# Five edits to a fused gated cross-attention and stream-mixing kernel: squares behind their loads, the high half of x from x itself, maxima one patch earlier, the last map in halves, and idle weights as output buffers

## The chip, the cores and the metric

The kernel runs on one core of one Trainium2 chip, as one program. The metric is device time in microseconds (us) of one execution. Before the change three runs took 1733.73, 1724.82 and 1726.72 us, so the median is 1726.72 us. One further execution was profiled; it took 1734.36 us, and the profile's span, from the first to the last instruction, is 1732.6 us.

The engines are named as in the profile: PE is the matrix engine (PEld its weight loads), DVE the vector engine, ACT the scalar engine, POOL the GpSimd engine and SP the queue that issues nearly all DMAs. Each of them works through its own instructions strictly in the order in which the program lists them.

## The reference

The input `x` is 8 batches of 512 rows by 2048 columns. Two blocks follow each other, each added to `x` with a gate:

```python
x = x + tanh(g_xattn) * xattn(layernorm(x), ctx, mask, Wq, Wk, Wv, Wo, biases)
x = x + tanh(g_ffn)   * ffn(layernorm(x), W_res, W_pre, W_post, bases, gate, W_branch)

def xattn(qk, v, masks):                 # per batch: 16 patches of 128 columns
    q, k = Wq @ qk + bq, Wk @ qk + bk    # 256 x 128 each, 8 heads of 32
    val  = Wv @ v + bv
    attn = softmax(q_h^T k_h / sqrt(32)) # 128 x 128 per head
    o    = gelu(val_h attn^T)            # exact gelu
    return (Wo @ o + bo) * masks

def ffn(x):                              # per row: 2048 columns = 4 streams of 512
    xn    = x * rsqrt(mean(x*x) + eps)
    H_res = sinkhorn(xn @ W_res.T + base, 50 iterations, tau 0.1)  # 4 x 4 per row
    H_pre, H_post = softmax(...), softmax(...)                     # 4 per row
    H_res = (1-g) * I + g * H_res
    y     = (sum_n H_pre[n] * x_n) @ W_branch
    return H_res @ x_streams + H_post * y
```

## The kernel before

**Steps.** The work is laid out in 128 steps `t`, one for each patch of 128 columns; four steps make a block `n` of 512 columns (`p` is the step within the block), four blocks a batch of 512 x 2048. The string `ORDER = "MeoaMgPlsMMvSMpOM"` is the order of the parts within a step, and `act(c, t)` runs the part of one letter. The parts that the change touches or that stand next to them:

- `s`: `smax(t + AHEAD)`, with `AHEAD = 3`. Eight products of a patch's queries and keys go into PSUM (L341), DVE takes the row maxima (L344, one reduction over 1024 columns), the maxima are split in two halves, turned by PE (L349), copied by ACT (`mh`, L351) and written by a DMA into rows 97 and 98 of the patch's query tile (L354). There they act as the subtracted maximum.
- `e`: `expo(t)`. The scores again, transposed and with the maxima in (L616), and their exponential on ACT (L618). `a`: `attv(t - 1)`, sums and products with the values. `g`, `o`, `O`: `outp`, gelu, output product, residual (L648 to L695).
- `p`: `proj(n + 2)`, the query and key projections. At `p == 0` the four 128 x 512 tiles of the block are normalised: POOL writes `xn = x * rstd + nb` (L271), ACT makes the 16-bit high half `h` from `xn` (L276), POOL the low half `l = xn - h` (L278). Afterwards twelve products for each of four row groups `m` (L289 to L291), and the result is written to DRAM (`qd`, L295).
- `stack(m)`: six DMAs (L308) and a mask row (L313) read `qd` back into one of `NS = 3` pairs of tiles `QS`, `KS`; one pair holds two patches. `stack(2n + 3)` is in the step `p == 2` (letter `P`), `stack(2n + 4)` at the end of the step `p == 3` (letter `p`).
- `S`: one step of `stats(b)`, the mean and variance of a later batch. Five pieces load 16 tiles of the transposed input (L577) and multiply them (L565); then the squares of x - mean are summed. For this 16 tiles are loaded (L597) and squared by ACT (L598), all sixteen in two pieces, each load followed by its square. All 32 tiles of a batch go through four buffers (`xTt`). With `EARLY = 4`, `stats(b)` starts at step t = 16 b - 20 for the batches from 2 on; batch 1 starts at t = 0.
- After a batch's last block, `ffn` makes the maps of all its 512 rows: a chain of 49 sweeps, each a product, a row sum and a reciprocal, twice (L865 to L875). For the batches 0 to 6 the two products of a sweep are on POOL and the rest on DVE; for batch 7 all is on DVE. `SPLITS` says in how many parts of the rows each operation of the chain is done.
- `mix`: the maps are applied, one quarter (128 rows) at a time. `mixv` does it on ACT, DVE and POOL (L964 to L975). `mixp` does it on PE; it is used for the twelve quarters that `PE_MIX` lists, of batches 4 to 7, and runs after step 128. Its outputs go from PSUM through a buffer `wp` (ACT, L1028) to DRAM (L1029). The buffers of `wp` are taken in turn from two pools: one buffer `eh` and two buffers `e32`.

**What sets the order.** The source gives the dependencies and an order of preference. When the program is built, a scheduler walks a simulated timeline and fixes the list of instructions of every engine, SP's list of DMAs included. So an edit in one part can shift the place of instructions of other parts. In the program before, the maxima of patch k + 3 always begin ahead of the scores of patch k + 1.

Of the kernel before, what the change touches and what calls it, by code (L numbers as in the profile page):

```python
# [9 lines left out]
F32 = mybir.dt.float32  # L10
# [3 lines left out]
AF = mybir.ActivationFunctionType  # L14
# [5 lines left out]
P = 128  # L20
# [5 lines left out]
BLK = 512  # L26
NBLK = S // BLK
# [4 lines left out]
NS = 3  # L32
HI = 1000
XPRE_POOL = lambda b: b < 7
AHEAD = 3
LXP = 1
SK_POOL = lambda b: b < 7
CT_ACT = False
XS_ACT = False
POOLMIX = lambda i, j: j == 1 and i > 0  # L40
BUF_GP = 1
BUF_OP = 1
BUF_XHP = 4
BUF_XNP = 2
BUF_XTP = 4
BUF_CTP = 2
BUF_QDP = 3
# [3 lines left out]
LASTN = 1  # L51
LASTM = 3
YS = True
EARLY = 4
LAGS = (30,) * 8
NV = 2
MIXN = 2
# [4 lines left out]
BUF_W = 2  # L62
# [3 lines left out]
BUF_EP = 2  # L66
BUF_XPRE = 1
PSTEPS = (0,1,1,2)
SP0 = 1
XH_POOL = lambda c: False  # L70
CAP = 1.0
NORM0 = True
D_MH = 0
# [3 lines left out]
D_ST = 0  # L77
BUF_XP = 20
PE_MIX = ((), (), (), (), (3,), (0, 1, 2, 3), (0, 1, 2, 3), (1, 2, 3))
SPLITS = (1, 1, 1, 1, 1, 1, 1, 1)  # L80
CHAINS = ((0,), (1,), (2,), (3,), (4,), (5,), (6,), (7,))
BUF_SK = 2
PE_IN = ((), (), (), (), (), (), (), ())
# [16 lines left out]
def gated_xattn_mhc_kernel(  # L100
# [21 lines left out]
    V, A, G, T, SY = nc.vector, nc.scalar, nc.gpsimd, nc.tensor, nc.sync  # L122
# [6 lines left out]
    def ctile(shape, dt, name):  # L129
        return const.tile(shape, dt, tag=name, name=name)  # L130
# [16 lines left out]
    WqkH = ctile([P, 4, 512], F16, "WqkH")  # L147
    WqkL = ctile([P, 4, 512], F16, "WqkL")
    Wv = ctile([P, 4, DK], F32, "Wv")
# [35 lines left out]
    xsp = ctx.enter_context(tc.tile_pool(name="xsp", bufs=2))  # L185
    xnp = ctx.enter_context(tc.tile_pool(name="xnp", bufs=BUF_XNP))
    xhp = ctx.enter_context(tc.tile_pool(name="xhp", bufs=BUF_XHP))
# [3 lines left out]
    ep = ctx.enter_context(tc.tile_pool(name="ep", bufs=BUF_EP))  # L191
# [6 lines left out]
    VF = [ctile([P, 2, DK], F32, f"VF{i}") for i in range(NV)]  # L198
# [5 lines left out]
    def defer(k, tag, fn):  # L204
        if k == 0:
            fn()
        else:
            late.append([k, fn, tag])
# [6 lines left out]
    def flush(which):  # L215
        for e in [e for e in late if which(e)]:
            late.remove(e)
            e[1]()
# [3 lines left out]
    rstd1 = {}  # L222
    nb1 = {}
# [28 lines left out]
    def finish_stats(b, nm, var):  # L252
        r = rsqrt(ln0, var, eps_ln, 4, "ln1")
        nb = ln0.tile([P, 4], F32, tag="nb1", name="nb1")
        V.tensor_tensor(nb, nm, r, ALU.mult)  # L255
        nmean[b], rstd1[b], nb1[b] = nm, r, nb
# [4 lines left out]
    def proj(n):  # L261

        b, k = divmod(n, NBLK)
        xt = xtile[n]
        hs, ls = [], []
        for c in range(4):
            xn = xnp.tile([P, BLK], F32, tag="xn", name="xn")
            if n == 0 and c > 1:
                A.activation(xn, xt[c], AF.Identity, scale=rstd1[b][:, c : c + 1], bias=nb1[b][:, c : c + 1])
            else:  # L270
                G.tensor_scalar(xn, xt[c], rstd1[b][:, c : c + 1], nb1[b][:, c : c + 1], ALU.mult, ALU.add)  # L271
            h = xhp.tile([P, BLK], F16, tag="xh", name="xh")
            if XH_POOL(c):
                G.tensor_copy(h, xn)
            else:
                A.copy(h, xn)  # L276
            l = xhp.tile([P, BLK], F16, tag="xl", name="xl")
            (V if n == 0 and c > 1 else G).tensor_tensor(l, xn, h, ALU.subtract)  # L278
            hs.append(h)
            ls.append(l)  # L280
        if NORM0:
            yield
        qd = qdp.tile([2, 4, 2, P, BLK], F16, tag="qd", name="qd")
        qds[n] = qd
        for m in range(4):
            ps = ps_p.tile([P, BLK], F32, tag="p", name="qk")
            ms = slice(m * P, (m + 1) * P)
            for c in range(4):
                T.matmul(ps, WqkH[:, c, ms], hs[c], start=(c == 0), stop=False)  # L289
                T.matmul(ps, WqkH[:, c, ms], ls[c], start=False, stop=False)  # L290
                mm = T.matmul(ps, WqkL[:, c, ms], hs[c], start=False, stop=(c == 3))  # L291
            ev = evp.tile([P, 2, BLK], F16, tag="ev", name="ev")
            ae = A.activation(ev[:, 0, :], ps, AF.Identity, bias=bqs[:, m : m + 1])  # L293
            ve = V.scalar_tensor_tensor(ev[:, 1, :], ps, bqs[:, m : m + 1], ev[:, 0, :], ALU.add, ALU.subtract)  # L294
            defer(D_QD, "qd", lambda m=m, ev=ev: SY.dma_start(qd[m // 2, 0:2, m % 2].rearrange("t p s -> p t s"), ev))  # L295
            if n == LASTN and m == LASTM:
                last.update(pe=mm, act=ae, dve=ve)
            yield
# [252 lines left out]
    fp = ctx.enter_context(tc.tile_pool(name="fp", bufs=2))  # L551
# [5 lines left out]
    def stats(b):  # L557

        lgs = xsp.tile([P, 512], F32, tag="lgs", name="lgs", bufs=1)
        for q4 in range(5):  # L560
            if q4 > 0:
                flush(lambda e: e[2] == "st")
                lg = ps_t.tile([P, 512], F32, tag="t", name="lgx")
                for g in range(4):
                    T.matmul(lg[32 * g : 32 * g + 32, :], Wm[:, 4 * q4 - 4 + g, :], xts[g], start=True, stop=True)  # L565
                if q4 == 1:
                    V.tensor_copy(lgs, lg)
                else:
                    V.tensor_tensor(lgs, lg, lgs, ALU.add)
            if q4 < 4:  # L570
                xts = []

                def ld(q4=q4, xts=xts):
                    for g in range(4):
                        xt_ = xtp.tile([P, 512], F32, tag="xTt", name="xTt")
                        k = 4 * q4 + g
                        SY.dma_start(xt_, xT[b, k * P : (k + 1) * P, :])  # L577
                        xts.append(xt_)

                defer(D_ST, "st", ld)  # L580
                yield 1
        rp = ps_t.tile([P, 4, 32], F32, tag="t", name="rawp")
        for c in range(4):
            T.matmul(rp[:, c, :], lgs[:, c * P : (c + 1) * P], sel, start=True, stop=True)
        rw = lnp.tile([P, 4, 32], F32, tag="rawx", name="rawx")
        V.tensor_copy(rw, rp)
        rawx[b] = rw
        if b == 0:
            return
        nm = ln0.tile([P, 4], F32, tag="nmean", name="nmean")  # L590
        V.tensor_scalar(nm, rw[:, :, NM], -1.0 / S, None, ALU.mult)
        yield 1
        sq = lnp.tile([P, 4, NBLK], F32, tag="sq1", name="sq1")
        for c in range(4):
            for k in range(NBLK):
                xs = xtp.tile([P, BLK], F32, tag="xTt", name="xs")
                (A if XS_ACT else SY).dma_start(xs, x[b, c * P : (c + 1) * P, k * BLK : (k + 1) * BLK])  # L597
                A.activation(xs, xs, AF.Square, bias=nm[:, c : c + 1], accum_out=sq[:, c, k : k + 1])  # L598
            if c % 2:
                yield 1  # L600
        var = lnp.tile([P, 4], F32, tag="var1", name="var1")
        V.tensor_reduce(var, sq, AX.X, ALU.add)
        V.tensor_scalar(var, var, 1.0 / S, None, ALU.mult)
        finish_stats(b, nm, var)
        yield 1
# [130 lines left out]
    def ffn(bs):  # L736
# [4 lines left out]
        tg = ""  # L741
        split = SPLITS[b - B]
        raw = f1.tile([P, NTM, 34], F32, tag="raw" + tg, name="raw", bufs=1)[:, :NT]
# [186 lines left out]
    def mixv(b, n, maps):  # L930
# [31 lines left out]
        for i in range(4):  # L962
# [12 lines left out]
            defer(D_OUT if live[0] else 0, "out", lambda i=i, w=w: SY.dma_start(out[b, n * P : (n + 1) * P, 512 * i : 512 * i + 512], w))  # L975
            yield 1

    def mixp(b, n, maps, inp=False):

        E, cst, pre, prc, post, rec, HR = maps  # L980
# [13 lines left out]
        xs = fp.tile([P, 512], F32, tag="xpre", name="xps", bufs=BUF_XPRE) if inp else xp_.tile([P, 512], F32, tag="xt", name="xps")  # L994
# [27 lines left out]
        for g in range(4):  # L1022
            q = 4 * n + g
            ps = ps_t.tile([P, 512], F32, tag="t", name="mx1") if inp else pw[g // 2][:, g % 2]
            T.matmul(ps, QD[:, 32 * g : 32 * g + 32].rearrange("p t i -> p (t i)"), ys, start=True, stop=False)
            T.matmul(ps, HD[:, g].rearrange("p t i -> p (t i)"), xc[g], start=False, stop=True)
            w = fp.tile([P, 512], F32, tag="w", name="w", bufs=BUF_W) if inp else ep.tile([P, 512], F32, tag="eh" if g % 2 else "e32", name="wp", bufs=1 if g % 2 else BUF_EP)
            A.activation(w, ps, AF.Identity, bias=rec[:, q, 2:3])  # L1028
            SY.dma_start(orow[q * P : (q + 1) * P, :], w)  # L1029
            yield 1  # L1030
# [7 lines left out]

    for t in range(2, AHEAD):
        smax(t)  # L1040
# [22 lines left out]
    def act(c, t):  # L1063
# [20 lines left out]
        elif c == "l" and live_:  # L1084
            if p == LXP and n > 1 and n + 3 < NTOT:
                load_x(n + 3)
        elif c == "s" and live_ and t + AHEAD < NT_:
            at("smax", smax, t + AHEAD)
        elif c == "v" and live_:
# [4 lines left out]
        elif c == "S" and live_:  # L1094
            if t == 0 and B > 1:
                sgens.append(stats(1))
            if t == min(8, NT_ - 6):
                sgens.append(stats(0))
            b2 = (t + EARLY) // 16 + 1
            if (t + EARLY) % 16 == 0 and 2 <= b2 < B:  # L1100
                sgens.append(stats(b2))
# [107 lines left out]
```

## Time and profile before

| | us |
|---|---|
| median of three runs | 1726.72 |
| the profiled execution | 1734.36 |
| its span | 1732.6 |
| PE busy | 1509.3 (87% of the span) |
| DVE busy | 1206.2 (70%) |
| ACT busy | 1059.5 (61%) |
| POOL busy | 817.8 (47%) |
| PE's mean granted clock | 0.948 |

A busy PE is not PE at its peak: its matmuls run at the clock that was granted, and the ends are modelled. The share of a line in the profile is an average over stages with different limits: the head (some 70 us, until the first exponential), the 128 steps (to about 1546 us), and the tail, where only maps and mixing are left. A wait is told as "engine and line that waited, engine and line that ended the wait: us in total, times, longest". Idle time of an engine that nobody waits for costs nothing.

### The profile page before, as it was taken

To read this page: it belongs to the slowest core of one execution; us is meant where nothing else is said; L and a number is where in the kernel's file an instruction comes from. 1 tells how busy PE (TensorE), PEld (TensorE's weight loads), DVE (VectorE), ACT (ScalarE), POOL (GpSimd) and SP (SyncE) were. 2 spreads that over 40 slices of the span, in tenths; PEclk is the share of its full clock that TensorE was granted. 3 is DMA by queue.
4 is the path that set the end of the run, shared out by engine and by line. 5 is a ranking of instruction groups with operands and counts; after the bars stand their busy time and mean duration, and the time that the engine had idled before them with its cause. 6 is when DMAs were issued, how large, how long until landed. Compare 5 with 4: busy or idle time off the path is not lost.

```text
span 1732.6 us, 32587 instructions
## 1 busy us (share of the span) xinstructions
PE 1509.3 (87%) x10517; PEld 884.2 (51%) x10517; DVE 1206.2 (70%) x3552; ACT 1059.5 (61%) x2042; POOL 817.8 (47%) x1158
## 2 busy tenths in 40 slices
PE   5898998999889888898789988897789879778887
PEld 2455555565556545555555555555456546542333
DVE  7534334575577577786877878886878888978872
ACT  3356457565656566667666577666766657654554
POOL 2323222444345445654567645565656654643211
PEclk9899999999899999999999999998989999889999
DMA  6788778568756874579566886678556665424443
GB/s 202 211 229 248 221 228 236 151 181 239 211 140 182 249 212 141 172 219 277 177 190 190 251 251 158 186 235 242 181 159 186 180 176 147 125 89 146 141 144 131
DMA packets 317657, 330.61 MB, mean 191 GB/s; under 512 B 50536, under 2 KB 215720, under 8 KB 317487
## 3 DMA queue, kind: packets, MB, share of 16 engines
q1 hardware_dynamic: 316238, 328.20, 64.7%
q8 instruction: 83, 1.36, 0.4%
q14 instruction: 88, 0.71, 0.1%
q10 hardware_dynamic: 1248, 0.33, 0.1%
HBM read 226.71 MB, written 101.16 MB: 189 GB/s over the span
## 4 chain that ended last, share of the span: by engine, by line
PE 43%; DMA 17%; DVE 16%; ACT 11%; issue 8%; POOL 4%; SPq 1%; POOLq 0%; ACTq 0%; DVEq 0%
PE vp L331 7%; DMA xs<-in_x_dram 5%; PE lgx L565 3%; PE qk L289 3%; DVE w L971 3%; PE qk L291 3%; PE qk L290 3%; PE op L688 3%; DMA out_dram<-w 3%; DMA x<-x1s 3%; PE op L689 2%; PE op L690 2%; PE smax L341 2%; PE u L637 2%; PE u L633 2%
## 5 line engine op out<-in xcount | busy, mean ns | idle before, releaser
L331 PE MATMUL vp<-Wv,ct 128*128 128x256 f32 x1024 | 257.8, 403 | 31.7 <-ACT VF L332 18.8
L871 POOL TENSOR_TENSOR W<-E,uv 128x64 f32<-128x64 f32 x343 | 117.1, 343 | 255.0 <-DVE uv L869 112.5
L331 PEld LDWEIGHTS vp<-Wv,ct 128*128 128x128 f32 x1024 | 200.0, 202 | 71.5 <-ACT VF L332 23.0
L278 POOL TENSOR_TENSOR xl<-xn,xh 128x512 f16<-128x512 f32 x126 | 153.1, 1224 | 128.9 <-ACT xh L276 128.4
L971 DVE SCALAR_TENSOR_TENSOR w<-x,Et,w 128x512 f32<-128x512 f32 x180 | 177.2, 985 | 43.7 <-POOL w L969 19.4
L289 PE MATMUL qk<-xh,WqkH 128*128 128x512 f16 x512 | 194.7, 381 | 11.5 <-DVE ev L294 8.9
L865 POOL TENSOR_TENSOR W<-E,uv 128x64 f32<-128x64 f32 x308 | 106.8, 348 | 195.6 <-DVE uv L875 95.9
L290 PE MATMUL qk<-xl,WqkH 128*128 128x512 f16 x512 | 194.7, 381 | 0.6 <-POOL xl L278 0.6
L291 PE MATMUL qk<-xh,WqkL 128*128 128x512 f16 x512 | 194.9, 381 | 0.0
L344 DVE TENSOR_REDUCE smax<-smax 128x8 f32<-128x1024 f32 x128 | 156.0, 1219 | 40.3 <-PE smax L341 22.5
L618 ACT ACTIVATE e<-sT,ebi,esc 128x1024 f32<-128x1024 f32 x128 | 153.3, 1197 | 32.4 <-PE sT L616 32.2
L688 PE MATMUL op<-gh,WoH 128*128 128x512 f32 x256 | 123.0, 482 | 33.0 <-DVE ev L294 23.7
L873 DVE TENSOR_REDUCE sm<-W 128x16 f32<-128x64 f32 x392 | 99.5, 255 | 62.8 <-POOL W L871 58.1
L694 ACT ACTIVATE junk<-xt,nmean 128x512 bf16<-128x512 f32 x128 | 91.7, 716 | 80.8 <-DVE xt L692 44.2
L294 DVE SCALAR_TENSOR_TENSOR ev<-qk,bqs,ev 128x512 f16<-128x512 f32 x128 | 93.4, 730 | 56.5 <-ACT ev L293 55.7
L293 ACT ACTIVATE ev<-qk,bqs 128x512 f16<-128x512 f32 x128 | 86.6, 678 | 74.0 <-PE qk L291 71.2
L271 POOL TENSOR_SCALAR xn<-xt,ln_r,nb 128x512 f32<-128x512 f32 x126 | 111.6, 889 | 33.1 <-DVE nb L255 25.5
L598 ACT ACTIVATE xs<-xs,nmean 128x512 f32<-128x512 f32 x112 | 79.9, 714 | 64.1 <-DMA xs<-in_x_dram 56.4
L341 PE MATMUL smax<-KS,QS 97*128 97x128 f16 x1024 | 86.3, 224 | 36.7 <-ACT mh L351 34.4
L692 DVE TENSOR_TENSOR xt<-op,xt 128x512 f32<-128x512 f32 x128 | 86.8, 678 | 42.0 <-PE op L691 40.9
L969 POOL TENSOR_TENSOR w<-w,pj 128x512 f32<-128x512 f32 x60 | 82.0, 1366 | 59.8 <-ACT w L964 42.7
L867 DVE TENSOR_REDUCE sm<-W 128x16 f32<-128x64 f32 x352 | 73.6, 210 | 51.2 <-POOL W L865 48.1
(288 smaller groups left out, 3559.2 us busy)
## 6 DMA issues: line engine op xcount, KB each, us to landing
xt<-in_x_dram SPq DMA_DIRECT2D x128, 256.0 KB
ct<-in_cx_dram SPq DMA_DIRECT2D x64, 512.0 KB
qd<-ev SPq DMA_DIRECT2D x128, 256.0 KB
xTt<-in_xT_dram SPq DMA_DIRECT2D x128, 256.0 KB
x1s<-xt SPq DMA_DIRECT2D x128, 256.0 KB
xs<-in_x_dram SPq DMA_DIRECT2D x112, 256.0 KB
QS<-qd SPq DMA_DIRECT2D x192, 128.0 KB
KS<-qd SPq DMA_DIRECT2D x192, 128.0 KB
```

Source lines behind the costliest of these rows:

```text
L271: G.tensor_scalar(xn, xt[c], rstd1[b][:, c : c + 1], nb1[b][:, c : c + 1], ALU.mult, ALU.add)
L278: (V if n == 0 and c > 1 else G).tensor_tensor(l, xn, h, ALU.subtract)
L289: T.matmul(ps, WqkH[:, c, ms], hs[c], start=(c == 0), stop=False)
L290: T.matmul(ps, WqkH[:, c, ms], ls[c], start=False, stop=False)
L291: mm = T.matmul(ps, WqkL[:, c, ms], hs[c], start=False, stop=(c == 3))
L331: T.matmul(ps[:, h, :], ct[:, c, h * P : (h + 1) * P], Wv[:, c, :], start=(c == 0), stop=(c == 3))
L341: T.matmul(sc[:, h, :], q[0:97, h, sl], kk[0:97, h, sl], start=True, stop=True)
L344: V.tensor_reduce(mx, sc, AX.X, ALU.max)
L618: A.activation(e32, sc, AF.Exp, bias=ebi[:, t : t + 1], scale=esc[:, t : t + 1])
L688: T.matmul(ps, WoH[:, e, cs], gh[:, e], start=(e == 0), stop=False)
L871: (G if SK_POOL(b - B + 8) else V).tensor_tensor(W4[:, h], E4[:, h], ub[:, h], ALU.mult)
L971: V.scalar_tensor_tensor(w, x1[j], E[:, n, 4 * j + i : 4 * j + i + 1], w, ALU.mult, ALU.add)
```

## The change

It has five parts.

1. In `stats`, two tiles are loaded in each piece and the two of the piece before are squared, so that the sixteen tiles take nine pieces in place of two (for batch 1, three of these make a step), and `EARLY` goes from 4 to 10, which starts `stats(b)` six steps sooner, at t = 16 b - 26.
2. The high half `h` is made by ACT straight from `x` with scale and bias, no longer from POOL's `xn`. `xn` has one buffer in place of two. The flags `XS_ACT` and `XH_POOL`, which were off, go.
3. `AHEAD` goes from 3 to 4: the maxima are taken a patch sooner. `NS` stays 3.
4. `SPLITS` of the last batch goes from 1 to 2: each operation of its chain is done in two halves of 32 columns that alternate.
5. `mixp` after step 128 takes its output buffers in turn from eight places: five are weights and value tiles that nobody reads any more by then, the others are those that it had.

```diff
@@ -32,16 +32,15 @@
-AHEAD = 3
+AHEAD = 4
...
-XS_ACT = False
...
-BUF_XNP = 2
+BUF_XNP = 1
...
-EARLY = 4
+EARLY = 10
...
-XH_POOL = lambda c: False
...
-SPLITS = (1, 1, 1, 1, 1, 1, 1, 1)
+SPLITS = (1, 1, 1, 1, 1, 1, 1, 2)
@@ -269,11 +267,9 @@
                 G.tensor_scalar(xn, xt[c], rstd1[b][:, c : c + 1], nb1[b][:, c : c + 1], ALU.mult, ALU.add)
+
             h = xhp.tile([P, BLK], F16, tag="xh", name="xh")
-            if XH_POOL(c):
-                G.tensor_copy(h, xn)
-            else:
-                A.copy(h, xn)
+            A.activation(h, xt[c], AF.Identity, scale=rstd1[b][:, c : c + 1], bias=nb1[b][:, c : c + 1])
             l = xhp.tile([P, BLK], F16, tag="xl", name="xl")
             (V if n == 0 and c > 1 else G).tensor_tensor(l, xn, h, ALU.subtract)
@@ -591,12 +587,18 @@
         sq = lnp.tile([P, 4, NBLK], F32, tag="sq1", name="sq1")
-        for c in range(4):
-            for k in range(NBLK):
+        loaded = []
+        for i in range(9):
+            now = loaded
+            loaded = []
+            for j in (2 * i, 2 * i + 1) if i < 8 else ():
+                c, k = divmod(j, NBLK)
                 xs = xtp.tile([P, BLK], F32, tag="xTt", name="xs")
-                (A if XS_ACT else SY).dma_start(xs, x[b, c * P : (c + 1) * P, k * BLK : (k + 1) * BLK])
+                SY.dma_start(xs, x[b, c * P : (c + 1) * P, k * BLK : (k + 1) * BLK])
+                loaded.append((c, k, xs))
+            for c, k, xs in now:
                 A.activation(xs, xs, AF.Square, bias=nm[:, c : c + 1], accum_out=sq[:, c, k : k + 1])
-            if c % 2:
+            if b > 1 or i % 3 == 2:
                 yield 1
@@ -975,6 +977,17 @@
+    spare = [WqkH.bitcast(F32)[:, 0:2, :], WqkL.bitcast(F32)[:, 0:2, :], Wv[:, 0:2, :], VF[0], VF[1]]
+    turn = [0]
+
+    def tailw(g):
+        k = turn[0] % (len(spare) + 3)
+        turn[0] += 1
+        if k < len(spare):
+            return spare[k].rearrange("p c e -> p (c e)")
+        return ep.tile([P, 512], F32, tag="eh" if k == len(spare) else "e32", name="wp", bufs=1 if k == len(spare) else BUF_EP)
+
     def mixp(b, n, maps, inp=False):
@@ -1024,7 +1037,7 @@
-            w = fp.tile([P, 512], F32, tag="w", name="w", bufs=BUF_W) if inp else ep.tile([P, 512], F32, tag="eh" if g % 2 else "e32", name="wp", bufs=1 if g % 2 else BUF_EP)
+            w = fp.tile([P, 512], F32, tag="w", name="w", bufs=BUF_W) if inp else tailw(g)
             A.activation(w, ps, AF.Identity, bias=rec[:, q, 2:3])
```

## The prediction

> **What bounds the kernel now.** I read the page first, then stretches, waits, groups, and the timeline of the tail.
>
> ```profile
> PE 1509.3 (87%) x10517; PEld 884.2 (51%) x10517; DVE 1206.2 (70%) x3552; ACT 1059.5 (61%) x2042; POOL 817.8 (47%) x1158
> ```
>
> PE is the bound, and 223 us of its span are idle. The change removes no matmul, so it can only move this idle time. The chain that ended last puts 5% of the span on "DMA xs", the loads of the squares, so I asked for the seven stretches in which squares run, and for what lies between them (columns: PE, PEld, DVE, ACT, POOL busy and instructions, PE clock, DMA share, GB/s):
>
> ```profile
> 410.00:447.00 37.00, 28.31 (x222) 19.31 (x223) 18.15 (x58) 24.85 (x56) 9.86 (x20) 0.86 0.81 235
> 1177.00:1217.00 40.00, 31.18 (x210) 19.00 (x210) 23.08 (x85) 25.53 (x61) 17.75 (x37) 0.87 0.76 221
> sum 256.00, PE 212.47 PEld 133.16 DVE 138.89 ACT 185.72 POOL 71.62; mean PE 30.35 PEld 19.02 DVE 19.84 ACT 26.53 POOL 10.23
> ```
>
> ```profile
> sum 1178.00, PE 1054.93 PEld 647.44 DVE 878.16 ACT 741.79 POOL 668.72; mean PE 150.70 PEld 92.49 DVE 125.45 ACT 105.97 POOL 95.53
> ```
>
> With squares PE is idle for 43.5 of 256 us (17.0%), between them for 123 of 1178 (10.4%). The waits name the places that the change touches:
>
> ```profile
> POOL xl L278 <- ACT xh L276: 128.4, 31, 26.4
> ...
> ACT xs L598 <- DMA xs<-in_x_dram: 56.4, 36, 6.1
> ```
>
> ```profile
> PE sT L616 <- DMA QS<-mh: 5.5, 2, 3.1
> ...
> PE sT L616 <- ACT mh L351: 3.6, 2, 3.0
> ...
> PE smax L341 <- DMA KS<-qd: 0.8, 1, 0.8
> ```
>
> ACT stands still for 56 us at squares, and what is queued behind them (exponentials, evacuations) reaches PE late. POOL's 128 us behind `xh` are long, but PE waits for `xh` and `xl` only 1.9 and 0.6 us. Maxima reach the scores with 9.1 us of PE waiting, and the maxima's own operands are in time: 0.8 us.
>
> **The change part by part.** The sum is made against the profiled execution (1734.4 us); that stands 7.6 us above the median of the runs, which I take off at the end.
>
> *Squares.* The same 112 loads and 112 squares remain. In the built list of ACT the squares stand in runs of at most four, where before runs of up to eight met four buffers, so that from the fifth on each waited for a load issued only after an earlier square. If the idle share falls from 17.0% to 10.4% of 256 us, 17 us go. The granted clock in the seven stretches, weighted, is 0.932 against 0.951 between them: 2% of 256 us, 5 more. Taken: -22; ends 0 and -43.5 (all idle time there). What is late next there is the evacuation of the projections (`op` L688 waits 23.7 us for `ev`). [...]
>
> `EARLY = 10` puts `stats(2)` beside the end of `stats(1)`, in the same four buffers; POOL already waits 25.5 us there once, for the statistics. In ACT's list these end behind the same exponential (the ninth) as before, so 0; ends -4 and +12 (half that wait). For the other batches they end 3 to 7 steps sooner, and nobody waits for them.
>
> *High half from x.* 128 casts go and 128 activations with scale and bias come:
>
> ```profile
> L276 ACT CAST xh<-xn 128x512 f16<-128x512 f32 x128 | 77.3, 612 | 15.3 <-POOL xn L271 8.7 <-PE qk L291 5.8
> ...
> L964 ACT ACTIVATE w<-x,sm,Et 128x512 f32<-128x512 f32 x80 | 64.1, 809 | 54.3 <-DMA out_dram<-w 45.3 <-DVE Et L894 5.3 <-DVE w L971 1.9
> ```
>
> ACT gets 128 x (809 - 612) = 25 us more. PE's waits that ACT ends add to some 80 us, 5% of the span, so +1; against it the 2.5 us of PE waiting for the halves go. Taken: -1; ends -5 and +12 (half of ACT's extra time on the path). The one buffer of `xn` costs nothing, since POOL writes and reads it in order; POOL's freed 128 us speed up sweeps that are not due.
>
> *Maxima a patch sooner.* At best the 9.1 us of waiting go; taken -6. But a pair of `QS`/`KS` still holds two patches of three pairs, so the maxima come closer behind the loads that they read. I added PE's busy time per instruction, line by line, along PE's built lists. From the scores that free a pair to the first maxima of the next filling (odd stacks) stood 23.1 us of PE work (median), and now 12.6; from a block's last projection to its first maxima (even stacks) 17.9, now 12.4. In the trace the last of the six loads lands 15.3 us (9.7 to 29.0) behind the freeing, and 11.8 us (7.8 to 19.7) behind the projection. With these landings 24 of 30 odd stacks would be late by 126 us in all, 10 of 30 even ones by 26. Yet the same count gives 26 us for the program before, where PE waited 0.8: real steps also hold idle time. And SP's new list has the odd loads in 6 to 8 successive places, where they lay over 6 to 14; at some 0.35 us an issue and with DMAs that wait in between, that is about 4 us sooner, and the odd sum falls to 59. So 59 + 26 - 26 = 59 us, of which I keep a quarter, because a PE that waits lets the other engines catch up and so loses waits of its own: +15. Behind a late `smax` the scores of the next patch are queued, and with them ACT's exponential. SP's queue is not blocked by it. Net taken: +9; ends -9 and +54 (half of 126 + 26 - 26, less 9).
>
> *Last map in halves.* 294 operations of DVE become 588. Alone, each waits for the one before:
>
> ```profile
> 1657.26 0.23 DVE L871 TENSOR_TENSOR W<-E,uv 128x64 f32<-128x64 f32 x1
> 1657.52 0.27 DVE L873 TENSOR_REDUCE sm<-W 128x16 f32<-128x64 f32 x1
> 1657.82 0.25 DVE L875 RECIPROCAL uv<-sm 128x16 f32<-128x16 f32 x1
> ```
>
> A sweep is 1.65 us. With the chain of batch 6 beside it, independent operations start before the one ahead has ended:
>
> ```profile
> 1573.04 0.26 DVE L873 TENSOR_REDUCE sm<-W 128x16 f32<-128x64 f32 x1
> 1573.22 0.21 DVE L865 TENSOR_TENSOR W<-E,uv 128x64 f32<-128x64 f32 x1
> 1573.35 0.25 DVE L875 RECIPROCAL uv<-sm 128x16 f32<-128x16 f32 x1
> 1573.51 0.17 DVE L867 TENSOR_REDUCE sm<-W 128x16 f32<-128x64 f32 x1
> ```
>
> At 0.10 to 0.14 us a half, twelve halves take 1.2 to 1.7 us: up to 10 us off the chain's last 50 us, where it runs alone; while both chains run (1568 to 1628 us, DVE 80% busy) 6 us may be lost. The chain ends at 1679, and PE gets to its maps at 1685 and loses 1.8 + 0.6 us there. Taken: -2; ends -2 and +6.
>
> *Idle weights.* ACT's waits for `wp` buffers are 3.8 us, and PE waits for none of them by name. Taken: -2; ends 0 and -4. The end itself stays: in PE's list `y` of the last `mixv` quarter still stands right ahead of the last eight mixing products, and its four outputs share two buffers:
>
> ```profile
> 1718.46 0.58 ACT L960 COPY xpre<-y 128x512 f32<-128x512 f32 x1 [2.00 <-PE y L928]
> ...
> 1722.01 0.81 ACT L964 ACTIVATE w<-x,sm,Et 128x512 f32<-128x512 f32 x1 [1.14 <-DMA out_dram<-w]
> ...
> 1729.67 0.33 SPq L975 DMA_DIRECT2D out_dram<-w  x1
> ```
>
> Sum: -22 + 0 - 1 + 9 - 2 - 2 = -18 us. 1734.4 - 18 - 7.6 = 1709 us.
>
> **The rivals.**
> - *Maxima wait for their loads (slower).* Landings stay as late as they are: +54 in place of +9, 1754 us. For it: 24 of 30 odd stacks. Against it: the tighter list of SP. It makes the kernel slower by 0.5% once the net of this part passes +36 us (the others sum to -27), that is 0.6 us for each of 62 stacks.
> - *Squares hidden.* The loads meet the DMA traffic of other steps, and PE's idle share there stays: -5 in place of -22, 1726 us. For it: DMA engines are 76 to 94% busy in these stretches, and the loads are as many. Against it: the runs of squares are shorter.
> - *Squares worth all idle time of their stretches.* -43.5 instead of -22: 1688 us. Against it: evacuations that PE waits for anywhere.
> - *Halves do not overlap (slower).* Twelve halves of about 0.19 us (between 0.15, the row of 128x4 operations, and 0.22) are 2.28 us a sweep, 0.63 more, 31 us over 49 sweeps; PE idles for it, less the 2 us credited: 1709 + 33 = 1742 us. The overlapping starts above speak against it. [...]
>
> **How the numbers follow.** 0.5% of 1726.7 us, 8.6 us, is about what a measurement of this kernel can tell from no change. Chances: forecast 0.40, all idle time 0.18, hidden 0.17, late loads 0.20, halves apart 0.05. Faster 0.58, same 0.17, slower 0.25. The range goes down to 1685 (just past the 1688 case) and up to 1750, which leaves out the upper half of the late loads and little else. As most of the chance is split over both signs, the forecast's own range is 1698 to 1718.
>
> **What would show it.** Right: ACT's wait for `xs` under 25 us; PE's idle share around squares near 10%; `smax` waiting for `KS` or `QS` loads under 20 us; POOL's wait for `xh` gone; `xh` near 810 ns; a sweep of batch 7, alone, near 1.3 us; the last output issued some 14 us behind the last `y`. The prediction is wrong if `smax` waits 40 us or more for its loads, if the squares' wait stays above 40 us, or if PE waits for batch 7's maps by more than 5 us.

## The result, and the profile after

| | before | after |
|---|---|---|
| median, us (four runs each) | 1727.59 | 1705.37 |
| lowest to highest, us | 1724.82 to 1733.73 | 1696.74 to 1706.40 |
| ratio to before, 95% interval | | 0.9848 [0.9819, 0.9877] |
| the profiled execution, us | 1734.36 | 1696.74 |
| its span, us; PE's mean granted clock | 1732.6; 0.948 | 1694.9; 0.962 |

The changed kernel is faster by 1.5%, 22 us between the medians, and the interval lies clear of 1. The prediction was 1709 us, with a range of 1685 to 1750. The two traces are 37.7 us apart, because the one before shows an execution slower than all four runs, and the one after the fastest of four; what is read from them is a division of the time, and the sizes come from the ratios.

The busy time of the engines on the page of the kernel after (columns: busy time, share of the span, instructions):

```profile
span 1694.9 us, 32856 instructions
...
PE 1479.0 (87%) x10452; PEld 877.8 (52%) x10517; DVE 1194.1 (70%) x3850; ACT 1081.4 (64%) x2051; POOL 819.0 (48%) x1158
```

PE is still the bound at 87%; 65 of its 10517 matmul records are missing from this trace. ACT has 22 us more, DVE's count has grown by the halves.

The waits that the prediction watched, from the view of waits of the kernel after (total us, times, longest):

```profile
POOL xl L274 <- ACT xh L272: 96.1, 20, 21.9
...
POOL xn L269 <- DVE nb L253: 57.9, 2, 32.8
...
ACT xs L600 <- DMA xs<-in_x_dram: 37.9, 27, 5.8
```

POOL's wait for `xh` was 128.4 us and is still 96.1; it was said to go. ACT's wait for the loads of the squares fell from 56.4 to 37.9, between the 25 that was to show the step right and the 40 that was to show it wrong.

PE's own waits after, same columns:

```profile
PE gTp L664 <- POOL o L655: 25.0, 6, 8.4
PE smax L345 <- DVE mq L343: 17.8, 9, 6.0
...
PE smax L337 <- DMA KS<-qd: 12.2, 8, 3.5
PE smax L337 <- ACT e L620: 12.0, 3, 7.9
...
PE smax L337 <- ACT mh L347: 2.1, 4, 1.1
```

The maxima now wait 12.2 us for their loads, where it was 0.8: the late loads that the prediction put on the path are there, and small. The last line is what matters most. In the program before it is the longest wait of PE, and the prediction did not use it:

```profile
PE smax L341 <- ACT mh L351: 34.4, 12, 7.3
```

The seven stretches in which squares run, after (columns: PE, PEld, DVE, ACT, POOL busy and instructions, PE clock, DMA share, GB/s):

```profile
360.00:402.00 42.00, 33.56 (x285) 22.41 (x290) 22.96 (x68) 30.97 (x69) 17.53 (x29) 1.00 0.85 241
...
sum 283.00, PE 229.26 PEld 144.73 DVE 163.49 ACT 220.65 POOL 122.74; mean PE 32.75 PEld 20.68 DVE 23.36 ACT 31.52 POOL 17.53
```

and what lies between them:

```profile
sum 1109.00, PE 1016.08 PEld 630.28 DVE 824.75 ACT 728.03 POOL 613.76; mean PE 127.01 PEld 78.79 DVE 103.09 ACT 91.00 POOL 76.72
```

Around the squares PE is idle for 53.7 of 283 us, 19.0%. That share was 17.0% and was to fall to about 10%: it did not fall. Between the stretches it went from 10.4% to 8.4% (92.9 of 1109 us). The windows before began some 8 us ahead of the first square, these some 4 us, and the last stretch before ran past the last exponential; cut as after, the shares before are 18.8% and 9.9%, which changes neither reading. So the total came out near the forecast, and the step that was to bring most of it failed in the trace. The experiments are about this.

### The profile page after: what moved, and what is told of

The parts are those of the page before. It is cut to its first block, busy times and chain, and to the rows that moved or that the text cites. A ratio compares the mean times of both kernels' runs of the same rounds, so it can differ in the third digit from the quotient of the medians.

```text
span 1694.9 us, 32856 instructions
## 1 busy us (share of the span) xinstructions
PE 1479.0 (87%) x10452; PEld 877.8 (52%) x10517; DVE 1194.1 (70%) x3850; ACT 1081.4 (64%) x2051; POOL 819.0 (48%) x1158
## 4 chain that ended last, share of the span: by engine, by line
PE 35%; DVE 21%; DMA 19%; ACT 10%; issue 8%; POOL 5%; SPq 2%; another core or an unknown queue 0%; POOLq 0%; ACTq 0%; DVEq 0%
DMA xs<-in_x_dram 5%; PE vp L327 5%; DVE w L973 4%; PE qk L285 2%; PE qk L286 2%; PE qk L287 2%; DMA out_dram<-w 2%; PE op L690 2%; PE lgx L561 2%; DMA qd<-ev 2%; DMA QS<-qd 2%; DVE w L976 2%; PE op L691 2%; PE u L635 2%; PE op L692 2%
## 5 line engine op out<-in xcount | busy, mean ns | idle before, releaser
L327 PE MATMUL vp<-Wv,ct 128*128 128x256 f32 x1024 | 248.9, 396 | 20.3 <-ACT VF L328 7.5
L274 POOL TENSOR_TENSOR xl<-xn,xh 128x512 f16<-128x512 f32 x126 | 156.0, 1238 | 111.2 <-ACT xh L272 96.1
L973 DVE SCALAR_TENSOR_TENSOR w<-x,Et,w 128x512 f32<-128x512 f32 x180 | 171.5, 954 | 43.5 <-POOL w L971 25.3
L867 POOL TENSOR_TENSOR W<-E,uv 128x64 f32<-128x64 f32 x308 | 105.3, 345 | 166.5 <-DVE uv L877 82.2
L875 DVE TENSOR_REDUCE sm<-W 128x16 f32<-128x64 f32 (+1 forms) x441 | 104.2, 242 | 59.2 <-POOL W L873 55.8
L269 POOL TENSOR_SCALAR xn<-xt,ln_r,nb 128x512 f32<-128x512 f32 x126 | 112.3, 891 | 67.5 <-DVE nb L253 57.9
L690 PE MATMUL op<-gh,WoH 128*128 128x512 f32 x256 | 118.1, 463 | 20.1 <-DVE ev L290 9.7
L869 DVE TENSOR_REDUCE sm<-W 128x16 f32<-128x64 f32 (+1 forms) x396 | 78.1, 203 | 58.5 <-POOL W L867 55.9
L337 PE MATMUL smax<-KS,QS 97*128 97x128 f16 x1024 | 83.7, 224 | 31.9 <-DMA KS<-qd 12.2
L600 ACT ACTIVATE xs<-xs,nmean 128x512 f32<-128x512 f32 x112 | 79.9, 714 | 42.5 <-DMA xs<-in_x_dram 37.9
```

Source lines behind the costliest of these rows:

```text
L327: T.matmul(ps[:, h, :], ct[:, c, h * P : (h + 1) * P], Wv[:, c, :], start=(c == 0), stop=(c == 3))
L690: T.matmul(ps, WoH[:, e, cs], gh[:, e], start=(e == 0), stop=False)
L867: (G if SK_POOL(b - B + 8) else V).tensor_tensor(W4[:, h], E4[:, h], vb[:, h], ALU.mult)
L973: V.scalar_tensor_tensor(w, x1[j], E[:, n, 4 * j + i : 4 * j + i + 1], w, ALU.mult, ALU.add)
```

## The experiments

Three theories. *The prediction's own terms* hold one by one: squares -22 us, maxima +9, the rest little. *The maxima a patch sooner bring the gain* (B where an expectation is about the maxima), and the squares bring little. And, formed after the first two sets: *the lists of the program before are an unlucky draw* of the scheduler (D), and any edit that makes new lists gains. In the expectations for the other parts the letters B and C stand for rivals of that part alone. The kernels of one set ran beside the same runs of the kernel before; all ratios are to it, with 95% intervals.

### One part taken back in the changed kernel

`u_ahead`: the maxima are taken as late as before.

```diff
-AHEAD = 4
+AHEAD = 3
```

> The changed kernel with AHEAD back at 3, all else changed. Theory A (the prediction's terms): the maxima a patch sooner cost 9 us net, so without it the kernel is at 0.985 x before less 9 us, a ratio of about 0.980 to the kernel before, and the 12 us in which PE waits at the maxima for KS and QS loads are gone. Theory B: the patch of distance is what gained, because the trace of the changed kernel has PE waiting for the copied maxima (mh) 2 us where it was 34 us; then this run is slower than the changed kernel, at a ratio of 0.990 or more, and that wait is back at 25 us or more.

Measured: 1717.11 us, 0.9915 [0.9884, 0.9945]. With `AHEAD = 4` the ratio is 0.9848. So inside this kernel the maxima a patch sooner are not a loss of 9 us; the gain reads as 0.7%, some 12 us, no more than a neutral edit moves this kernel (below). PE's wait for `mh` came back to 13.0 us only, not to the 25 that theory B asked for.

`u_squares`: squares in two pieces, `EARLY` as before.

```diff
-EARLY = 10
+EARLY = 4
...
-        loaded = []
-        for i in range(9):
-            now = loaded
-            loaded = []
-            for j in (2 * i, 2 * i + 1) if i < 8 else ():
-                c, k = divmod(j, NBLK)
+        for c in range(4):
+            for k in range(NBLK):
...
-            if b > 1 or i % 3 == 2:
+            if c % 2:
```

> The changed kernel with the squares in two pieces behind their loads again and EARLY = 4. Theory A: the squares were worth 22 us, so the gain is all but gone: ratio 0.997 (0.994 to 1.0), and ACT's wait for xs is back above 50 us. Theory B: as PE's idle share around the squares has not fallen in the changed kernel's trace (19% there, as before), they were worth little: ratio within 0.003 of the changed kernel's 0.985.

Measured: 1697.73 us, 0.9832 [0.9788, 0.9876]. Without the part that was priced at -22 us the kernel is as fast as with it. ACT's wait for `xs` is 38.4 us, as in the kernel after (37.9), where theory A expected more than 50. `EARLY` alone, with the squares in nine pieces, was not tried.

`u_xh`: the high half is cast from `xn` again, which has two buffers.

```diff
-BUF_XNP = 1
+BUF_XNP = 2
...
-            A.activation(h, xt[c], AF.Identity, scale=rstd1[b][:, c : c + 1], bias=nb1[b][:, c : c + 1])
+            A.copy(h, xn)
```

> The changed kernel with the high half cast from xn again and two buffers for xn. Theory A: worth 1 us, ratio 0.985 as for the changed kernel (0.982 to 0.988). Theory B: POOL and ACT no longer pass each tile back and forth, which brings the low halves and POOL's sweeps earlier: ratio 0.990 or more, and POOL's wait for xh is back from 96 us to some 128 us.

Measured: 1687.35 us, 0.9765 [0.9735, 0.9795], the fastest of all kernels here. Both theories missed: it is faster, and POOL's wait for `xh` stays at 96.3 us. The edit takes back two things, the activation and the single buffer of `xn`. The group of `xh` in its list of ACT's groups, and below it that of the kernel after:

```profile
L272 ACT CAST xh<-xn 128x512 f16<-128x512 f32 x128 | 76.8, 611 | 18.7 <-POOL xn L269 15.3 <-PE qk L287 2.5
```

```profile
L272 ACT ACTIVATE xh<-xt,nb,ln_r 128x512 f16<-128x512 f32 x128 | 98.5, 803 | 8.8 <-PE qk L287 8.5
```

`u_split`: the chain of the last batch in one part.

```diff
-SPLITS = (1, 1, 1, 1, 1, 1, 1, 2)
+SPLITS = (1, 1, 1, 1, 1, 1, 1, 1)
```

> The changed kernel with the last map in one part. Theory A: worth 2 us, ratio 0.986, and PE waits in the tail for batch 7's maps by up to 3 us. Theory B (halves start too close to each other to overlap, or cost the chain of batch 6 its time): without them the tail is shorter, ratio below 0.983.

Measured: 1697.62 us, 0.9825 [0.9795, 0.9855]; no loss. The ratio is what theory B asked for, but the tail, from the last exponential to the end, is 215.0 us in its trace and 215.8 in that of the kernel after.

### One part alone in the program before

`o_ahead`:

```diff
-AHEAD = 3
+AHEAD = 4
```

> The kernel before with AHEAD = 4 and nothing else. Theory B (the maxima's distance is the main gain, as taking it back cost 11 us): ratio 0.990 or less to the kernel before, and PE's wait for mh at the maxima, 34 us before, is under 10 us. Theory C (it gains only together with another part, such as the squares or the idle weights): ratio 0.997 or more.

Measured: 1696.38 us, 0.9822 [0.9792, 0.9852]: one constant gives 30.7 us (1.78% of 1726.7), as much as all five parts or more. What PE waits for `mh`, at the scores and at the maxima, in its view of waits:

```profile
PE sT L616 <- ACT mh L351: 11.8, 10, 3.0
...
PE smax L341 <- ACT mh L351: 2.7, 3, 1.1
```

At the maxima the wait fell from 34.4 to 2.7 us, at the scores it rose from 3.6 to 11.8.

`o_squares`: only the nine pieces and `EARLY = 10` (the reverse of the diff of `u_squares`, on the program before).

```diff
-EARLY = 4
+EARLY = 10
...
-        for c in range(4):
-            for k in range(NBLK):
+        loaded = []
+        for i in range(9):
...
-            if c % 2:
+            if b > 1 or i % 3 == 2:
```

> The kernel before with the squares a piece behind their loads and EARLY = 10, and nothing else. The prediction's term: -22 us, ratio 0.987. Theory B (taking them back from the changed kernel cost nothing, 0.983 against 0.985): ratio between 0.995 and 1.005, although ACT's wait for xs falls from 56 us to 45 or less.

Measured: 1697.09 us, 0.9822 [0.9791, 0.9853]. Alone, the squares gain 30.7 us as well, more than either theory said. Its waits of ACT, and then of PE:

```profile
ACT xs L604 <- DMA xs<-in_x_dram: 26.1, 17, 5.2
```

```profile
PE smax L341 <- ACT mh L351: 15.8, 10, 4.4
```

`o_xh`: only the high half from `x`; `xn` keeps its two buffers.

```diff
-            if XH_POOL(c):
-                G.tensor_copy(h, xn)
-            else:
-                A.copy(h, xn)
+            A.activation(h, xt[c], AF.Identity, scale=rstd1[b][:, c : c + 1], bias=nb1[b][:, c : c + 1])
```

> The kernel before with the high half made from x (xn keeps two buffers), and nothing else. The prediction's term: -1 us, ratio 0.999. Theory B (taking it back from the changed kernel gained 14 us, so the 25 us of extra ACT time are on the path for a good half): ratio 1.004 to 1.010. Theory C (it is the single buffer of xn that costs, not the activation): ratio 1.000 or less.

Measured: 1711.89 us, 0.9918 [0.9885, 0.9950], a gain of 14 us, where theories A and B had none. PE's wait:

```profile
PE smax L338 <- ACT mh L348: 20.2, 8, 6.0
```

`u_tailw`, in the same set: the changed kernel with the output buffers of before.

```diff
-            w = fp.tile([P, 512], F32, tag="w", name="w", bufs=BUF_W) if inp else tailw(g)
+            w = fp.tile([P, 512], F32, tag="w", name="w", bufs=BUF_W) if inp else ep.tile([P, 512], F32, tag="eh" if g % 2 else "e32", name="wp", bufs=1 if g % 2 else BUF_EP)
```

> The changed kernel with the three old output buffers after step 128. Theory A: worth 2 us, ratio 0.986. Theory B: since squares, high half and halves gained nothing on their own, the idle weights must carry what the maxima's 11 us leave of the gain, up to 12 us: ratio 0.989 or more and a tail longer by 5 us or more than the 217 us of the changed kernel's trace.

Measured: 1702.16 us, 0.9856 [0.9821, 0.9890]. The idle weights bring nothing that can be told from the scatter.

So three parts that have little to do with each other gain 1.8%, 1.8% and 0.8% alone and 1.5% together. Either each removes the same loss, or each only shuffles an unlucky list. The next set tells these apart.

### New lists without a change of meaning

`n_stack`: the program before with the loads of the keys listed ahead of those of the queries. The work is the same; the scheduler makes new lists.

```diff
-        for dst, side, parts in ((QS[i], 0, (0, 1, 0)), (KS[i], 1, (0, 0, 1))):
+        for dst, side, parts in ((KS[i], 1, (0, 0, 1)), (QS[i], 0, (0, 1, 0))):
```

> The kernel before, with the six loads of a filling of QS and KS listed keys first instead of queries first: the same instructions, the same loads, no part of the change; but the scheduler's lists differ from there on. Theory D (the lists of the kernel before are a poor draw, and any edit that has them made anew gains some 1.5%, as three unlike parts each did alone): ratio 0.990 or less. Theory B/C (the parts gain by what they do): ratio between 0.995 and 1.005.

Measured: 1732.18 us, 1.0004 [0.9987, 1.0022].

`n_order2`: the program before with two letters of the order of a step exchanged.

```diff
-ORDER = "MeoaMgPlsMMvSMpOM"
+ORDER = "MeoaMgPlsMMvMSpOM"
```

> The kernel before, with one piece of mixing listed ahead of the statistics' piece of its step instead of behind it: the same instructions, new lists. Theory D: ratio 0.990 or less. Theory B/C: between 0.995 and 1.005.

Measured: 1742.98 us, 1.0059 [1.0040, 1.0078].

`o_tail`: the program before with the two parts of the tail (halves and idle weights).

```diff
-SPLITS = (1, 1, 1, 1, 1, 1, 1, 1)
+SPLITS = (1, 1, 1, 1, 1, 1, 1, 2)
...
+    spare = [WqkH.bitcast(F32)[:, 0:2, :], WqkL.bitcast(F32)[:, 0:2, :], Wv[:, 0:2, :], VF[0], VF[1]]
...
+            w = fp.tile([P, 512], F32, tag="w", name="w", bufs=BUF_W) if inp else tailw(g)
```

> The kernel before with the last map in halves and the idle weights as output buffers, and nothing else; every engine's list is that of the kernel before until after step 128. Theory A: these are worth 4 us, ratio 0.998. Theory B: up to 12 us, ratio 0.993, with the tail shorter than 211 us. Theory D: 1.000, and the maxima's wait for mh stays at 34 us.

Measured: 1733.39 us, 1.0013 [0.9995, 1.0030].

`n_stack_a`: the edit of `n_stack` on the changed kernel.

> The changed kernel, with the loads of QS and KS listed keys first: the same instructions, new lists. Theory D: any draw lies some 1.5% under the kernel before, with a scatter of half a per cent, so ratio 0.976 to 0.992; if it is 0.980 or less, taking back the high half (0.9765) is within the scatter of lists and its 14 us are no price of the activation. Theory B/C: within 0.003 of 0.985.

Measured: 1691.01 us, 0.9782 [0.9750, 0.9814], where the changed kernel had 0.9848.

In two draws new lists alone do not make the program before faster, so D falls as far as two draws can show. They keep its wait, as the views of waits of `n_stack`, `n_order2` and `o_tail` show in this order:

```profile
PE smax L341 <- ACT mh L351: 25.5, 8, 7.3
```

```profile
PE smax L341 <- ACT mh L351: 35.9, 11, 7.8
```

```profile
PE smax L337 <- ACT mh L347: 34.6, 14, 6.7
```

They also give a measure of scatter: a neutral edit moved the one program by 0.0 and 0.6% and the other by 0.7%. `n_stack_a` came out under the 0.980 that its expectation named, so by it the 0.9765 of `u_xh` lies within the scatter of lists. Differences of that size between single kernels here, such as 0.9825 or 0.9915 against 0.9848, say nothing of the part that was taken back.

### The shared loss

What the three parts share is seen in one stretch of the program before, from its timeline (start, us, engine, line, operation, and in brackets the idle time of the engine ahead of it and what ended it; SPq issues DMAs):

```profile
1196.36 0.72 ACT L598 ACTIVATE xs<-xs,nmean 128x512 f32<-128x512 f32 x1 [1.71 <-DMA xs<-in_x_dram]
...
1197.08 0.70 ACT L598 ACTIVATE xs<-xs,nmean 128x512 f32<-128x512 f32 x1
1197.19 3.83 SPq L597 DMA_DIRECT2D xs<-in_x_dram  x3
...
1199.86 0.72 ACT L598 ACTIVATE xs<-xs,nmean 128x512 f32<-128x512 f32 x1 [1.99 <-DMA xs<-in_x_dram]
...
1200.84 0.24 ACT L351 COPY mh<-smax 16x128 f16<-16x128 f16 x1
...
1201.13 1.01 PE L341 MATMUL smax<-KS,QS 97*128 97x128 f16 x8 [6.68 <-ACT mh L351]
```

`smax` ends with a copy by ACT, `mh` (L351), that reads the PSUM buffer of the maxima. Maxima and scores (L339, L614) take turns in two such buffers (the pool `ps_s`, L194), so the next of them on PE waits for `mh`. Here `mh`, 0.24 us long, is queued on ACT behind a run of squares that wait for loads, and PE stands for 6.68 us. Compared by source line, 1802 of the 2042 operations of ACT in this trace (the other 240 read its accumulators) and 3540 of the 3552 of DVE (all but its memsets) start in the order in which the built program lists them.

For each kernel I took PE's waits of 0.6 us or more that `mh` ended, looked at what ACT ran in them, and summed those with a square in them:

| kernel | PE waits for `mh`, us | of these with squares ahead on ACT, us | ratio |
|---|---|---|---|
| before | 36.5 | 24.5 | 1 |
| n_order2 | 38.6 | 25.5 | 1.0059 |
| o_tail | 34.5 | 23.2 | 1.0013 |
| n_stack | 26.6 | 22.4 | 1.0004 |
| o_xh | 22.0 | 12.8 | 0.9918 |
| u_ahead | 13.0 | 4.8 | 0.9915 |
| u_squares | 16.4 | 8.3 | 0.9832 |
| o_squares | 15.7 | 0.6 | 0.9822 |
| o_ahead | 12.5 | 8.4 | 0.9822 |
| u_tailw | 2.3 | 0 | 0.9856 |
| after | 2.9 | 1.1 | 0.9848 |
| u_split | 2.8 | 0 | 0.9825 |
| n_stack_a | 0.8 | 0 | 0.9782 |
| u_xh | 15.5 | 5.8 | 0.9765 |

The four kernels at 1 or above have 22 to 26 us of it, `o_xh`, which gains 0.8%, has half, and all that gain 1.4% or more have 0 to 8. `u_ahead` does not fit: it has 4.8 us and gains only 0.9%; it is taken up below with the high half. Nor does this wait put the fastest in order: `u_xh` has more of it than the kernel after. The reading is that shorter runs of squares take away what `mh` is queued behind, that maxima a patch sooner leave PE other work, so that it does not come to the buffer so soon, and that both thus remove one loss, which can be removed once. The four long ones of the five waits (4.0 to 7.3 us) cost more than themselves, because the granted clock was 0.50 behind them. The same stretch in windows of 3.41 us (columns as in the windows above; the clock is the third column from the right):

```profile
1191.78:1195.19 3.41, 1.79 (x34) 0.95 (x30) 2.80 (x14) 0.82 (x2) 1.88 (x7) 1.00 0.88 302
1195.19:1198.60 3.41, 0.00 (x0) 0.00 (x0) 0.52 (x3) 1.52 (x4) 0.60 (x2) 1.00 0.98 333
1198.60:1202.02 3.42, 0.89 (x8) 0.84 (x8) 0.00 (x0) 2.16 (x5) 0.00 (x0) 0.50 0.80 246
1202.02:1205.43 3.41, 2.15 (x12) 1.57 (x10) 3.15 (x12) 3.41 (x10) 0.65 (x3) 0.50 0.27 82
1205.43:1208.84 3.41, 3.41 (x9) 2.35 (x8) 3.05 (x13) 3.29 (x9) 1.48 (x6) 0.50 0.65 224
1208.84:1212.26 3.42, 3.42 (x25) 2.05 (x24) 2.38 (x6) 0.93 (x3) 1.25 (x2) 1.00 0.76 209
```

PE gets half the clock from 1198.6 to 1208.8 us, 7.7 us of it after the wait has ended. With the half-rate stretches at the other three long waits (6.2, 7.1 and 3.4 us behind them) that is 24.4 us at half rate; half of it, 12.2 us, is my estimate of what was lost. 24.5 + 12.2 = 36.7 us is the most that this loss can be; 30.7 is what `AHEAD` or the squares alone gave. That both parts work through it rests on the wait's fall and on the gains that do not add; it is not shown.

The trace of `o_squares` speaks in part against it. The seven stretches of squares, from 4 us ahead of the first square to 2 us behind the last, in the program before, in `o_ahead` and in `o_squares`:

```profile
sum 228.00, PE 185.04 PEld 117.55 DVE 123.28 ACT 158.05 POOL 54.41; mean PE 26.43 PEld 16.79 DVE 17.61 ACT 22.58 POOL 7.77
```

```profile
sum 226.00, PE 195.82 PEld 125.08 DVE 128.72 ACT 162.51 POOL 58.41; mean PE 27.97 PEld 17.87 DVE 18.39 ACT 23.22 POOL 8.34
```

```profile
sum 264.00, PE 218.29 PEld 138.59 DVE 154.62 ACT 212.14 POOL 122.22; mean PE 31.18 PEld 19.80 DVE 22.09 ACT 30.31 POOL 17.46
```

PE's idle time there falls from 43.0 to 30.2 us in `o_ahead`, but in `o_squares` it is 45.7 us, in longer stretches. There the wait for `mh` went and others came: over the whole trace the maxima wait 10.5 us for `KS` loads (0.8 before), and PE waits 22.7 us for POOL's `o` (10.0 before). What fell in `o_squares` is the idle time between the stretches, from 116 to 99 us (`o_ahead`: 106), and time lost at half rate: span times (1 - clock), averaged over the runs, is 14.7 us less than in the runs of the kernel before beside them, 18.1 us less in `o_ahead`. That is half or more of either gain. Why the steps between the squares got faster is open. `EARLY`, which moves the statistics, was not tried apart from the squares. Nor was the direct test made: only `mh` taken off ACT, or a third buffer for maxima and scores.

## Why the prediction was right, and where it was not

The time, the sign and the range were right, but the sum by luck: two of its terms were wrong in opposite directions.

- *Maxima a patch sooner, +9.* This is the step with the wrong sign: -30.7 us alone; in the changed kernel it reads as -12, within the scatter. The price of late loads, +15, was about right (12.2 us of `smax` waiting for `KS`). The other side, "At best the 9.1 us of waiting go", counted only the scores that wait for maxima. It left out 34.4 us in which the next maxima wait for the buffer that `mh` releases, though that line stood first among PE's waits.
- *Squares, -22 between 0 and -43.5.* Alone -30.7 us, within the ends. In the changed kernel 0: the term was priced as if it stood alone, and with `AHEAD = 4` most of the wait is gone without it (8.3 us in `u_squares`, 24.5 before). The reading "If the idle share falls from 17.0% to 10.4%" failed: it is 19.0%, and in `o_squares`, alone, 17.3% (45.7 of 264 us), where the same cut gives 18.8% before. I took the idle time there for late evacuations; 24.5 us of it was PE's wait for `mh` behind the squares. Without its 5 us for the clock the term would have been -17; alone it was almost twice that.
- *The clock, 5 us within the squares' term.* Too small. Span times (1 - clock) is 89 us before and 65 after in the traces, 25 of the 37.7 us between them; over runs it averages 74 us after (four runs) and 89 to 92 us in the three sets of runs of the kernel before beside the experiments, some 16 us apart, where the medians are 22 us apart. Of 231 windows of 3.413 us at full rate in which PE's busy share was under 0.4, 230 were followed by half rate (last section), so I count this as no second cause; idle time here cost more than itself.
- *High half from x, -1 between -5 and +12.* Per operation as said: 803 ns against 810 predicted, and 128 x (803 - 612) = 24 us more for ACT. Alone it gains 14 us, little more than the 0.6% that a neutral edit moved; there the wait behind the squares is half, 12.8 us in place of 24.5, how was not shown. Where that wait is small, it seems to cost: 0.9848 against 0.9765 with the cast (`u_xh`), and 0.9915 (`u_ahead`) against 0.9822 (`o_squares`, which lacks the tail's parts too), 14 and 16 us. The pairs agree, but a neutral edit moved this kernel by 0.7%, and both pairs change the single buffer of `xn` as well, which was not tried alone: neither the cost nor its cause is shown. POOL's wait for `xh` did not go, since `xl` needs `xh`, and ACT makes that behind its own queue. Its fall from 128.4 to 96.1 us is not this part's: `u_xh` has 96.3 and `o_squares` 96.1, both with the cast.
- *EARLY, 0.* Not tried alone. POOL waits 57.9 us for the statistics where it waited 25.5, but that does not follow `EARLY`: `o_squares`, with 10, has 28.2, `u_squares`, with 4, has 52.5, and the neutral `n_stack`, with 4, 54.5. PE's wait for POOL's `o` rose from 10.0 to 25.0 us; it is 22.7 in `o_squares` and 19.4 in `n_stack`, so that this is not told apart from the lists either.
- *Halves and idle weights, -2 each.* 0 together: 1.0013 [0.9995, 1.0030]. The halves do overlap, as the rows of before said. A sweep of the last batch alone, in the kernel after, begins at L867 and again 1.40 us later, against 1.65 before and 1.3 predicted:

```profile
1621.04 0.18 DVE L867 TENSOR_TENSOR W<-E,uv 128x32 f32<-128x32 f32 x1
...
1621.28 0.17 DVE L869 TENSOR_REDUCE sm<-W 128x8 f32<-128x32 f32 x1
1621.39 0.19 DVE L867 TENSOR_TENSOR W<-E,uv 128x32 f32<-128x32 f32 x1
1621.50 0.19 DVE L871 RECIPROCAL uv<-sm 128x8 f32<-128x8 f32 x1
...
1622.44 0.19 DVE L867 TENSOR_TENSOR W<-E,uv 128x32 f32<-128x32 f32 x1
```

  In `o_tail` the chain ends 151.9 us behind the start of the last exponential, in the program before 157.4. The time stays, because these are 5 us off a chain that PE hardly waits for: at its maps PE's mixing (`mx`) waited 1.8 and 0.6 us before, and 2.3 us in the kernel after. In the kernel after, the end is as the prediction had it, with four outputs through two buffers behind the last `y`:

```profile
1684.35 0.81 ACT L966 ACTIVATE w<-x,sm,Et 128x512 f32<-128x512 f32 x1 [1.10 <-DMA out_dram<-w]
...
1689.79 2.57 SPq L977 DMA_DIRECT2D out_dram<-w  x2
```

  The last issue ends 11.6 us behind the last `y` (1680.76 us), as before (1730.0 and 1718.43), where the prediction said some 14.

The rivals: *maxima wait for their loads* is refuted by 12.2 us (its price was 54, its limit 40). *Halves do not overlap* is refuted by the sweep and by `o_tail`; in the rows above a half starts at 1621.39 us, 0.06 us before the one ahead has ended. *All idle time of the squares' stretches* fell with the share of 19.0%. *Squares hidden* came true in the changed kernel, where the squares bring nothing; its reason, other DMA traffic, does not explain that they gain 30.7 us alone, and a second part that removes the same wait would.

By the runs, the sum would be: one shared wait -31, the high half +14 if that is real, the tail 0: -17 with it and -31 without, against -22 measured, and the neutral edits say that 10 us of such a sum is the draw of the lists.

## What to carry to other kernels

Look first at the longest wait of the bounding engine and ask what stands queued ahead of the releaser on its engine: a copy of 0.24 us behind squares that wait for loads kept this kernel's PE waiting for 24.5 us, and by estimate up to 12 us more was lost at half rate behind it. Then look whether idle time fell where the wait stood: in `o_squares` the wait went and the idle time there stayed. Before adding up the parts of a change, ask which of them remove the same wait, and price that once. Where a scheduler makes the lists, run a neutral edit or two, so that the scatter of lists is known before parts are told apart by less than it.

## What the runs showed of the hardware

In the traces before and after, the stretches in which PE was granted 0.50 of its clock, 28 and 26 of them, begin in each trace on one grid of 3.413 us. I cut all 14 traces into consecutive windows of 3.413 us, on the grid on which the half-rate stretches of each trace begin, left out the first 60 us, and counted windows at full rate by PE's busy share in them and by whether the next window was at half rate:

| PE busy in the window | windows | next at half rate |
|---|---|---|
| under 0.4 | 231 | 230 |
| 0.4 to 0.5 | 141 | 95 |
| 0.5 to 0.6 | 195 | 25 |
| 0.6 and more | 5572 | 16 |

Twelve of the 16 in the last row are one place in the head, where PE makes 32 products of 32 columns each (`ws`, L524 in the program before, 3.9 us). PE counts as busy there, and half rate followed all the same.

Two cases, before and after, as windows:

```profile
1021.10:1024.50 3.40, 1.67 (x12) 1.17 (x10) 3.32 (x15) 3.40 (x11) 0.99 (x2) 1.00 0.94 283
1024.50:1027.90 3.40, 3.40 (x10) 1.16 (x8) 2.29 (x6) 3.31 (x6) 3.40 (x5) 0.50 0.98 330
1027.90:1031.30 3.40, 3.40 (x16) 2.32 (x15) 1.97 (x5) 3.40 (x11) 2.91 (x4) 0.99 0.65 224
```

```profile
1006.00:1009.41 3.41, 1.22 (x28) 0.95 (x28) 3.41 (x6) 2.59 (x5) 2.13 (x3) 1.00 1.10 317
1009.41:1012.83 3.42, 3.21 (x15) 2.34 (x8) 2.92 (x22) 3.04 (x6) 1.37 (x4) 0.51 0.85 216
1012.83:1016.24 3.41, 3.41 (x18) 2.21 (x17) 2.44 (x7) 3.36 (x5) 2.11 (x3) 1.00 0.05 11
```

In the first, PE was busy for 1.67 of 3.40 us, its longest gap was 1.20 us, and the next window ran at half rate: 1.7 us more lost, by the same estimate. The half-rate stretches last one to four such windows (the last of each trace runs past the span), 181 us in all before and 131 after. Of the 26 windows before that were followed by half rate, 16 met no idle gap of PE as long as 3.413 us, and 14 of the 22 after.

What half rate did to products is seen in the program before, in the window that begins at 1567.24 us: the eight products of 512 columns (`yp`, L926 to L928) from 1567.59 to 1570.58 us start 0.42 to 0.43 us apart, where the two at full rate at 1564.91 us start 0.23 us apart.
